# One tile for the edge buffers, and 34 gathers of a layer that take only the first rows of their block

## The chip, the cores and the metric

The kernel runs on one core of a Trainium2 chip. The metric is device time in microseconds (us) of one execution. Before the change it is 3410.35 us, the median of three runs (3400.02 to 3417.9). The profiled execution, a run of its own, took 3422.3 us, of which the profile's span covers 3420.5.

## The reference, cut to what matters

A graph of 6250 nodes with 128 features and 100,000 directed edges; each node has one of 16 types, each edge one of 32. Two layers of typed graph attention, then one linear layer, a residual and a layer norm:

```python
def gt_layer(x, ntype, etype, src, dst, Wk, Wq, Wv, Wa, Watt, Wmsg, pri, skip, g, b):
    k, q, v = (typed_linear(x, ntype, W).reshape(n, H, HS) for W in (Wk, Wq, Wv))
    kT = jnp.einsum('nhd,htdo->nhto', k, Watt)
    vT = jnp.einsum('nhd,htdo->nhto', v, Wmsg)
    a = jnp.einsum('ehd,ehd->eh', kT[src, :, etype], q[dst]) * pri[:, etype].T / SQRT_D
    att = edge_softmax(a, dst, n)
    hag = segment_sum((vT[src, :, etype] * att[:, :, None]).reshape(-1, H * HS), dst, n)
    h = silu(typed_linear(hag, ntype, Wa))
    alpha = sigmoid(skip[ntype])[:, None]
    return layer_norm(h * alpha + x * (1.0 - alpha)) * g + b
```

H is 8 heads of HS = 16. A softmax runs over the edges that arrive at one node, 16 of them on average.

## The kernel before

**Tables.** For each layer a table in device memory holds, for every node and edge type, one row of 256 numbers (1 KB): key and value after the edge type's matrices. PE makes it in pieces of 128 nodes by 16 edge types (`table_block`, L384), ScalarE and in part VectorE copy the pieces out of PSUM into `st` (L391, L389), and GpSimd (POOL in the profile) scatters each piece with an indirect DMA, rows of 16 KB (L537 for layer 0, L1997 for layer 1).

**Blocks and slots.** The nodes are sorted on the chip (`rank_order`): into four classes of four node types each, within a class by falling degree, and cut into blocks of 128 nodes, one node to a partition. Each block has a fixed number of slots, at most one edge of each node to a slot: 25, 21, 19, 18, 17, 16, 15, 15, 14, 12, 11 for the eleven blocks of a class (`OWN_SLOTS`) and 42, 20, 16, 14, 9 for five mixed blocks (`MIXED_SLOTS`), which take the nodes that found no room in their class. The first mixed block has 26 slots of its own and 2 that are shared. Since nodes are sorted by degree, a block's last slots are used by the nodes of its first partitions alone. `ell` holds for each node and slot the table row of its edge, fetched with one gather per block (L1139). In `limits_of`, `room` gets each block's number of slots by a memset (L1230), and if a degree is above it, `over` is set; the program then takes a general path, which walks the edges one at a time (`arm(False)`), in place of the fast one.

**The fast path's order.** `edges` runs once per layer over 16 superblocks of one to four blocks. A block's slots are cut into chunks of at most four (`CH`). Per chunk: `kv`, a buffer of 128 partitions by four slots by 256 numbers, one of 12 in a rotating pool (L1718); one indirect gather for each slot (L1722), which fetches 128 table rows by a column of `ell`; the product of the keys with the query (L1738, VectorE, all four slots at once, in place) and its sum per head into `a` (L1744). A block later the generator `finished` adds `neg`, which is -1e30 where a node has no edge in the slot, takes the softmax, weighs the values in place and adds them up over chunks (`kv<-kv,wq`, `acc<-kv,acc`); the last of these instructions gives the buffer back. 819 gathers a layer, 1638 in all.

**What sets the order.** In the fast path GpSimd's instructions stand in the written order. Those of the other engines are ordered by the framework, from dependencies, its own estimates and the edges drawn with `behind`: work of the nodes (`on.vector` and the like) stays behind the stream instruction that was written before it. That node work (typed linear layers, layer norm, next queries) and the pieces of the second table are generators, and `tick` advances them between chunks. GpSimd's queue thus holds gathers, the scatters of the second table (layer 0) and the scatters of the output (L2035, layer 1). A tile's dependencies and semaphores are drawn by the framework.

Of the kernel before, what the change touches and what calls it, by code (L numbers as in the profile page):

```python
# [9 lines left out]
F32 = mybir.dt.float32  # L10
# [4 lines left out]
ALU = mybir.AluOpType  # L15
# [4 lines left out]
P = 128  # L20
# [8 lines left out]
NC = 4  # L29
# [3 lines left out]
CH = 4  # L33
# [2 lines left out]

PIECE = 6


def bins_of_degrees(lam):  # L40

# [3 lines left out]

OWN_SLOTS = (25, 21, 19, 18, 17, 16, 15, 15, 14, 12, 11)
MIXED_SLOTS = (42, 20, 16, 14, 9)

# [27 lines left out]
def kernel(  # L78
# [21 lines left out]
    nc = tc.nc  # L100
    N, D = out.shape
# [11 lines left out]
    CB, MB = len(OWN_SLOTS), len(MIXED_SLOTS)  # L113
    KB = list(OWN_SLOTS) * NC + list(MIXED_SLOTS)
    NB = len(KB)
    MIXED0 = NC * CB * P
    NR = NB * P
    TOP = NC * CB
    GB = [OWN + REST if b == TOP else KB[b] for b in range(NB)]
    KO = [sum(GB[:b]) for b in range(NB)]  # L120
    KS = sum(GB)
# [21 lines left out]
    tabs = [dram.tile([(NR if l else NP) * RT, 2 * D], F32, name=f"tab{l}") for l in range(L)]  # L143
# [10 lines left out]
    ell = keep.tile([P, KS], I32, name="ell")  # L154
# [242 lines left out]
    pp = prep.enter_context(tc.tile_pool(name="prep", bufs=1))  # L397
# [26 lines left out]
    rowf = pp.tile([P, 1], F32, name="rowf")  # L424
# [73 lines left out]
    for e in range(AHEAD):  # L498
        nc.gpsimd.indirect_dma_start(
            out=xa[:, e, :], out_offset=None, in_=x,  # L500
            in_offset=bass.IndirectOffsetOnAxis(ap=ahead[:, e:e + 1], axis=0))
    nc.vector.tensor_tensor(toward, toward, firstmost.unsqueeze(2).to_broadcast([P, AHEAD, NT]),
                            op=ALU.not_equal)
# [4 lines left out]
    for tg in range(TG):  # L508
        nc.vector.tensor_scalar(ahead_rows[:, tg], ahead_f, float(TG), float(tg),
                                op0=ALU.mult, op1=ALU.add)  # L510
# [74 lines left out]
    for i in range(2):  # L585
# [5 lines left out]
                                 op0=ALU.mult, op1=ALU.add)  # L591
# [31 lines left out]
    for c0, i0 in enumerate(cuts[:3]):  # L623
# [11 lines left out]
        for i in range(sl.start, sl.stop):  # L635
            nc.vector.tensor_scalar(row1[:, i - i0], colb, placef[:, i:i + 1], None,
                                    op0=ALU.is_equal)
        for i in range(sl.start, sl.stop):
# [6 lines left out]
                            op0=ALU.mult, op1=ALU.add)  # L645
# [45 lines left out]
    for tg in range(TG):  # L691
        nc.vector.tensor_scalar(rows1[:, tg], place2, float(TG), float(tg),
                                op0=ALU.mult, op1=ALU.add)
# [9 lines left out]
                            op0=ALU.is_gt)  # L703
# [155 lines left out]
    with tc.If(unsorted > 0):  # L859
# [7 lines left out]
        with tc.For_i(0, EC, 1) as j:  # L867
# [7 lines left out]
                out=c0, out_offset=None, in_=cnt[:],  # L875
                in_offset=bass.IndirectOffsetOnAxis(ap=pair[:, 0:1], axis=0))
# [27 lines left out]
                out=cnt[:], out_offset=bass.IndirectOffsetOnAxis(ap=to[:, 0:1], axis=0),  # L904
                in_=c1, in_offset=None)
            nc.gpsimd.indirect_dma_start(
                out=order[:], out_offset=bass.IndirectOffsetOnAxis(ap=pos[:, 0:1], axis=0),
                in_=pair, in_offset=None)
# [9 lines left out]
    for r in range(N * RT, NR * RT, P):  # L918
        n = min(P, NR * RT - r)
        nc.sync.dma_start(tabs[1][r:r + n, :], zeros[:n])  # L920

    with tc.manual_schedule(engines={mybir.EngineType.Pool, *engines}):
# [246 lines left out]
        def limits_of(meta, full, rest_at):  # L1169
# [59 lines left out]
            for b in range(NB):  # L1229
                nc.vector.memset(room[:, b:b + 1], float(KB[b]))  # L1230
                if b % 4 == 3:
                    yield
            two = pp.tile([P, 2], F32, name="two")
            nc.vector.tensor_tensor(room, degr, room, op=ALU.is_gt)
            nc.vector.tensor_reduce(two[:, 0:1], room, axis=AX.X, op=ALU.max)
# [125 lines left out]
    def arm(fast):  # L1361
# [4 lines left out]
            on.hold()  # L1366

        outs_put, results = [], []
        STB = 3 if fast else 2
        ep = ctx2.enter_context(tc.tile_pool(name="ep", bufs=2))  # L1370
        npl = ctx2.enter_context(tc.tile_pool(name="npl", bufs=1))
        eps = npl.tile([P, 1], F32, name="eps")
        nc.vector.memset(eps, LN_EPS)
# [101 lines left out]
        def edges(l):  # L1475
# [201 lines left out]
            for s, (i0, k, types) in enumerate(sbs):  # L1677
                asked = None
                if s + 1 < len(sbs):
                    asked = queries(got, *sbs[s + 1])  # L1680
                    spread(work, asked, 24 if mixed(s + 1) else 11 if l == 0 else 8, asking(s))
                sums = ep.tile([P, SB, D], F32, name="sums")
                den = ep.tile([P, SB, H], F32, name="den")
                for i in range(k):
                    b = i0 + i
                    K = KB[b]
                    a = ep.tile([P, max(KB), H], F32, name="a")
                    own = OWN if b == TOP else K
                    chunks = [(j, min(j + CH, own)) for j in range(0, own, CH)]
                    if b == TOP:  # L1690
                        chunks.append((OWN, OWN + REST))
                    kvt = []
                    then = []

                    def steps():

                        for _ in range(2 if s + 2 >= len(sbs) else 1):
                            step()

                    def step(end=False):  # L1700

                        if next(before, then) is then and not then:
                            if i + 1 < k:
                                then.append(query(s, i + 1))
                            elif asked and (end or work == [] or all(w[0] is not asked
                                                                     for w in work)):
                                rush(work, asked)
                                then.append(query(s + 1, 0))

                    cut = 0  # L1710
                    if b == sbs[-1][0] + sbs[-1][1] - 1:
                        cut = (K - 2 * CH) // CH
                        assert cut > 0 and (K + 1) * H <= 2 * D and K < max(KB)
                    for j0, j1 in chunks:
                        c = j1 - j0
                        if b == sbs[-1][0] + sbs[-1][1] - 1 and j1 > K - 2 * CH:
                            closing.append(b)
                        kv = ep.tile([P, CH, 2 * D], F32, name="kv", bufs=12)  # L1718
                        kvt.append(kv)
                        for j in range(j0, j1):  # L1720
                            at = KO[b] + j
                            get = nc.gpsimd.indirect_dma_start(  # L1722
                                out=kv[:, j - j0, :], out_offset=None, in_=tabs[l][:],
                                in_offset=bass.IndirectOffsetOnAxis(ap=ell[:, at:at + 1], axis=0))
                            gathered[0] = True
                            if l == 1:
                                for put in puts:
                                    after(get, put, "rows of the table")
                                puts.clear()
                            elif at == KO[sbs[0][0]]:  # L1730
                                for load in load_next(nc.sync):
                                    after(load, get, "the first table goes first")
                        kk = kv[:, :c, :D]
                        rest = b == TOP and j0 == OWN
                        if rest:
                            moved(rows_of, got[s][0][:, i, :], kv[:, 2, :D])
                        of = kv[:, 2, :D] if rest else q
                        stream[nc.vector] = nc.vector.tensor_tensor(  # L1738
                            kk, kk, of.unsqueeze(1).to_broadcast([P, c, D]), op=ALU.mult)
                        steps()  # L1740
                        tick(c / 3)
                        to = (kv[:, 3, D:D + c * H].rearrange("p (k h) -> p k h", h=H) if rest
                              else a[:, j0:j1, :])
                        nc.vector.tensor_reduce(to, kk.rearrange("p k (h d) -> p k h d", h=H),  # L1744
                                                axis=AX.X, op=ALU.add)
                        if rest:
                            nc.vector.tensor_tensor(
                                kv[:, 3, :RK * c * H].rearrange("p (r c) -> p r c", r=RK),
                                nth.unsqueeze(2).to_broadcast([P, RK, c * H]),
                                kv[:, 3, D:D + c * H].unsqueeze(1).to_broadcast([P, RK, c * H]),  # L1750
                                op=ALU.mult)
                        if cut and len(kvt) == cut:
                            for _ in before:
                                pass
                            before = finished(s, i, chunks[:cut], kvt[:cut], a, sums, den,
                                              (0, j1))
                        steps()
                        tick(c / 3)
                        steps()
                        tick(c / 3)  # L1760
                        leave()
                    for _ in before:
                        pass
                    if not then:
                        step(end=True)
                    before = finished(s, i, chunks[cut:], kvt[cut:], a, sums, den,
                                      (chunks[cut][0], K) if cut else None)
                    q = then[0] if then else None
# [345 lines left out]
        if not fast:  # L2114
            for i0, k in superblocks(NT):
                n = k * P
# [87 lines left out]
```

## Time and profile before

| what | value |
|---|---|
| median of three runs | 3410.35 us |
| profiled execution | 3422.3 us |
| its span | 3420.5 us |
| busy: PE, DVE (VectorE), ACT (ScalarE), POOL (GpSimd) | 1793.1, 1867.6, 1019.3, 1975.8 us |
| gathers of L1722 | 1638, 1565.8 us busy |
| DMA | 672.23 MB, mean 197 GB/s |

A row of a group of instructions names line, engine, operation, output and inputs, count, busy time, mean duration in ns of one, and after the second bar the idle time of the engine just before them with what ended it ("issue" is time in which the engine waited for nothing that the profile shows, "remote" an event of which it knows no source). A row of waits names who waited, for whom, the total in us, how often, and the longest. A row of the timeline has start, duration, engine, line, operation, tiles and, in brackets, the idle time before it. A row of a line's own view gives the smallest, the median and the largest duration in ns. Many of VectorE's and PE's instructions stand under line 299, a helper, so they are told apart by their tiles. "PEld" is PE's weight load, "PEclk" the granted clock of TensorE.

### The profile page before, as it was taken

What the parts mean: (1) busy time and instruction counts of PE and PEld (TensorE: products, weight loads), DVE (VectorE), ACT (ScalarE), POOL (GpSimd) and SP (SyncE); (2) the same over time, 40 slices, a digit from 0 to 9 for tenths busy, and PEclk for the clock granted to TensorE, in tenths of its full rate; (3) what the DMA queues carried; (4) which work ended last, traced back from release to release, by engine and by line L of the source; (5) the groups of instructions that cost most, each with busy time, mean ns of one, the idle gap of its engine ahead of it and who ended that gap; (6) DMA issues with size and microseconds to landing.
All of it is one profiled execution on the core that took longest, in us unless ns stands there. A gap on an engine that the chain in (4) does not pass through costs nothing. (4 is left out here: it accounts for less than half of the span.)

```text
span 3420.5 us, 22378 instructions
## 1 busy us (share of the span) xinstructions
PE 1793.1 (52%) x5496; PEld 818.3 (24%) x5496; DVE 1867.6 (55%) x4420; ACT 1019.3 (30%) x2089; POOL 1975.8 (58%) x2123
## 2 busy tenths in 40 slices
PE   6999896118867678586877784011122103120122
PEld 3444333003324223232333342000011001010011
DVE  6576554446446555465555443456545645664566
ACT  5887343003432344333444453000101100010111
POOL 3334655665655655566656443756666566657664
PEclk8998766556667666776656675555555555555555
DMA  8999999335664566556767577323223333323231
GB/s 287 427 423 395 381 406 349 111 87 206 231 225 171 191 243 225 199 199 231 254 248 257 215 276 270 105 86 93 88 86 102 92 88 95 97 87 104 86 91 53
DMA packets 151156, 672.23 MB, mean 197 GB/s; under 512 B 35520, under 2 KB 67554, under 8 KB 125922
## 3 DMA queue, kind: packets, MB, share of 16 engines
q0 software_dynamic: 113472, 635.98, 51.8%
q1 hardware_dynamic: 32850, 31.51, 3.1%
q10 hardware_dynamic: 4688, 3.15, 0.4%
q8 instruction: 48, 0.79, 0.1%
q14 instruction: 98, 0.80, 0.1%
HBM read 245.49 MB, written 429.22 MB: 197 GB/s over the span
## 5 line engine op out<-in xcount | busy, mean ns | idle before, releaser
L1722 POOL DMA_INDIRECT kv<-tab,ell x1638 | 1565.8, 956 | 777.5 <-issue 461.5
L391 ACT COPY st<-tb 128x512 f32<-128x512 f32 x1371 | 727.4, 606 | 721.0 <-PE tb L384 397.1
L384 PE MATMUL tb<-bd,kvT 32*128 32x512 f32 x1538 | 591.4, 898 | 116.9 <-ACT st L391 62.9
L1738 DVE TENSOR_TENSOR kv<-kv,wq 128x512 f32<-128x512 f32 (+3 forms) x446 | 283.2, 637 | 242.1 <-DMA kv<-tab,ell 108.4
L299 PE MATMUL nb<-xm,wqa 128*128 128x384 f32 (+3 forms) x528 | 286.5, 703 | 166.8 <-issue 72.4
L1744 DVE TENSOR_REDUCE a<-kv 128x32 f32<-128x512 f32 (+3 forms) x446 | 282.4, 635 | 150.2 <-remote 95.8
L384 PEld LDWEIGHTS tb<-bd,kvT 32*128 32x128 f32 x1538 | 218.4, 246 | 351.3 <-issue 171.5
L299 DVE SCALAR_TENSOR_TENSOR xm<-ntb,nb 128x512 f32<-128x512 bf16 (+3 forms) x320 | 156.9, 543 | 229.0 <-remote 111.3
L1997 POOL DMA_INDIRECT tab<-st,row x98 | 97.1, 991 | 305.0 <-ACT st L391 224.0
L384 PE MATMUL tb<-bd,vT 32*128 32x512 f32 x800 | 250.6, 776 | 25.2 <-ACT st L391 10.6
L299 PE MATMUL nb<-xm,wkqv 128*128 128x384 f32 (+3 forms) x528 | 219.2, 572 | 65.9 <-issue 28.8
L299 DVE TENSOR_TENSOR acc<-kv,acc 128x512 f32<-128x512 f32 (+3 forms) x346 | 219.3, 634 | 62.7 <-remote 39.9
L299 PE MATMUL nb<-ident,hag 128*128 128x128 f32 x98 | 27.5, 417 | 406.3 <-DVE kv L1738 225.7
L299 PE MATMUL nb<-by,all_rows 49*128 49x512 bf16 (+3 forms) x32 | 14.5, 453 | 416.5 <-DVE kv L1738 207.0
L537 POOL DMA_INDIRECT tab<-st,rows x92 | 95.2, 1035 | 211.0 <-ACT st L391 178.5
L384 PE MATMUL tb<-bd,kT 32*128 32x512 f32 x800 | 212.5, 769 | 4.6 <-DVE st L389 4.1
L299 PEld LDWEIGHTS nb<-xm,wqa 128*128 128x128 f32 x528 | 134.6, 282 | 334.2 <-issue 204.9
L299 DVE TENSOR_TENSOR kv<-kv,wq 128x512 f32<-128x512 f32 (+3 forms) x334 | 207.7, 623 | 2.0 <-issue 2.0
L389 DVE COPY st<-tb 128x512 f32<-128x512 f32 x182 | 119.1, 686 | 111.9 <-PE tb L384 65.0
L299 PEld LDWEIGHTS nb<-xm,wkqv 128*128 128x128 f32 x528 | 112.7, 232 | 185.6 <-issue 92.5
L299 ACT ACTIVATE wq<-a 128x120 f32<-128x120 f32 (+12 forms) x98 | 28.4, 290 | 374.7 <-DVE xm L299 85.1
L1525 ACT COPY wq<-hq 128x128 f32<-128x128 f32 x49 | 13.1, 268 | 395.3 <-DVE acc L299 215.6
(387 smaller groups left out, 2020.8 us busy)
## 6 DMA issues: line engine op xcount, KB each, us to landing
kv<-tab,ell POOLq DMA_INDIRECT x1638
hq<-hqx SPq DMA_DIRECT2D x7, 768.0 KB
hqx<-hs SPq DMA_DIRECT2D x7, 512.0 KB
hq<-hqx SPq DMA_DIRECT2D x5, 576.0 KB
hqx<-xr SPq DMA_DIRECT2D x10, 256.0 KB
hqx<-hs SPq DMA_DIRECT2D x5, 384.0 KB
hr<-hqx SPq DMA_DIRECT2D x7, 256.0 KB
tab<-st,row POOLq DMA_INDIRECT x98
```

Of the source, the lines that this page charges most:

```text
L299: put = issue(*args, **kwargs)
L384: stream[nc.tensor] = nc.tensor.matmul(pt, yT[s, i * P:(i + 1) * P], bd[s, tt, :], start=True, stop=True)
L389: nc.vector.tensor_copy(to, pt)
L391: stream[nc.scalar] = nc.scalar.copy(to, pt)
L537: put = nc.gpsimd.indirect_dma_start(out=tabs[0].rearrange("(n t) c -> n (t c)", t=16), out_offset=bass.IndirectOffsetOnAxis(ap=rows_of_pi ...
L1525: nc.scalar.copy(standing["wq"][:, at:at + D], got[s][0][:, i, :])
L1722: get = nc.gpsimd.indirect_dma_start(out=kv[:, j - j0, :], out_offset=None, in_=tabs[l][:], in_offset=bass.IndirectOffsetOnAxis(ap=ell[:, ...
L1738: stream[nc.vector] = nc.vector.tensor_tensor(kk, kk, of.unsqueeze(1).to_broadcast([P, c, D]), op=ALU.mult)
L1744: nc.vector.tensor_reduce(to, kk.rearrange("p k (h d) -> p k h d", h=H), axis=AX.X, op=ALU.add)
L1997: put = nc.gpsimd.indirect_dma_start(out=tabs[1].rearrange("(n t) c -> n (t c)", t=16), out_offset=bass.IndirectOffsetOnAxis(ap=row2[:, tg ...
```

## The change

The twelve `kv` buffers become one tile `ring` of 48 slots, `RING * CH`; a chunk takes the next four in turn, counted by `fed` over both layers. Two tables of bounds name a block and a slot and give how many of the block's first nodes may use it: 7 for each of the four classes and 6 for the mixed blocks, 34 in all. In these slots a gather takes only that many rows (48 to 112, multiples of 16) and leaves the other partitions of the slot as they were; the first time that a slot of the ring is used, it takes all 128. In `limits_of` each bound lowers `room` by one for the nodes from the bound on, so that a node that would need such a slot sets `over`.

```diff
+RING = 12
...
+FEW = {(0, 22): 112, (0, 23): 80, (0, 24): 48, (1, 20): 112, (7, 14): 96, (8, 13): 112, (10, 10): 112}
+FEW_MIXED = {(1, 17): 112, (1, 18): 112, (1, 19): 112, (2, 13): 96, (2, 14): 96, (2, 15): 96}
...
+    few = {(c * CB + b, j): n for c in range(NC) for (b, j), n in FEW.items()}
+    few.update(((NC * CB + b, j), n) for (b, j), n in FEW_MIXED.items())
...
+            beyond = pp.tile([P, 1], F32, name="beyond")
+            for (b, j), n in few.items():
+                if b < CB or b >= TOP:
+                    nc.vector.tensor_scalar(beyond, rowf, float(n), None, op0=ALU.is_ge)
+                    nc.vector.tensor_tensor(room[:, b:b + 1], room[:, b:b + 1], beyond,
+                                            op=ALU.subtract)
+            for c in range(1, NC):
+                nc.vector.tensor_copy(room[:, c * CB:(c + 1) * CB], room[:, :CB])
+            yield
...
+        fed, filled = [0], set()
...
+        ring = ep.tile([P, RING * CH, 2 * D], F32, name="ring", bufs=1) if fast else None
...
-                        kv = ep.tile([P, CH, 2 * D], F32, name="kv", bufs=12)
+                        chunk = fed[0] % RING
+                        fed[0] += 1
+                        kv = ring[:, chunk * CH:(chunk + 1) * CH]
...
+                            n = few.get((b, j), P)
+                            if (chunk, j - j0) not in filled:
+                                filled.add((chunk, j - j0))
+                                n = P
                             get = nc.gpsimd.indirect_dma_start(
-                                out=kv[:, j - j0, :], out_offset=None, in_=tabs[l][:],
-                                in_offset=bass.IndirectOffsetOnAxis(ap=ell[:, at:at + 1], axis=0))
+                                out=kv[:n, j - j0, :], out_offset=None, in_=tabs[l][:],
+                                in_offset=bass.IndirectOffsetOnAxis(ap=ell[:n, at:at + 1], axis=0))
```

More of the change, by code (lines that the diff above doesn't have):

```diff
@@ L118 @@
     TOP = NC * CB
+    few = {(c * CB + b, j): n for c in range(NC) for (b, j), n in FEW.items()}
+    few.update(((NC * CB + b, j), n) for (b, j), n in FEW_MIXED.items())
+    assert all(n % 16 == 0 and j < KB[b] and (b, j - 1) not in few or few[b, j - 1] >= n
+               for (b, j), n in few.items())
+    assert all(j == KB[b] - 1 or (b, j + 1) in few for b, j in few)
     GB = [OWN + REST if b == TOP else KB[b] for b in range(NB)]
```

## The prediction

> **What bounds the kernel now.** I read the busy times by stage first, then the gathers' own line, then GpSimd's and VectorE's waits stage by stage, then the timeline at the places where a stage turns or ends. The stages are the preparation with the first table (0 to 580 us), the edges of layer 0 beside the second table (580 to 2080) and the edges of layer 1 (2080 to the end):
>
> ```profile
> core 0: us, PE busy (x) PEld busy (x) DVE busy (x) ACT busy (x) POOL busy (x), PEclk, DMA share, GB/s
> 0.00:580.00 580.00, 502.65 (x2189) 232.88 (x2189) 344.58 (x827) 341.61 (x669) 263.27 (x338) 0.81 0.96 386
> 580.00:2080.00 1500.00, 1044.39 (x2735) 461.99 (x2736) 783.52 (x1790) 543.93 (x1104) 876.23 (x914) 0.66 0.60 212
> 2080.00:3420.50 1340.50, 246.03 (x577) 123.40 (x571) 739.49 (x1805) 133.76 (x317) 836.28 (x872) 0.53 0.33 97
> ```
>
> The preparation is held by the DMA engines (share 0.96). In the other two stages no engine looks full. POOL's busy time leaves out what lies between its instructions, so I read that from the timeline:
>
> ```profile
> 1105.55 0.95 POOL L1722 DMA_INDIRECT kv<-tab,ell  x1 [0.30 <-issue]
> 1106.80 0.95 POOL L1722 DMA_INDIRECT kv<-tab,ell  x1 [0.30 <-issue]
> ...
> 2819.39 0.94 POOL L1722 DMA_INDIRECT kv<-tab,ell  x1 [10.18 <-DVE t L299]
> ```
>
> Gathers that wait for nothing start every 1.25 us: 0.95 in the instruction and 0.30 that always lies between two. With 0.30 for each instruction POOL is taken for 876.2 + 914 x 0.30 = 1150 of the 1500 us of layer 0 (77%) and for 836.3 + 872 x 0.30 = 1098 of the 1340.5 us of layer 1 (82%). It is the fullest engine of both, and what it lacks is waits such as the third line: a gather stood 10.18 us because VectorE had not yet let go of the buffer. By kind, layer 0 and then layer 1:
>
> ```profile
> POOL kv L1722 <- issue: 219.4, 718, 0.8
> POOL tab L1997 <- ACT st L391: 216.7, 40, 15.1
> POOL kv L1722 <- DVE acc L299: 75.8, 20, 16.2
> ```
> ```profile
> POOL kv L1722 <- issue: 225.4, 739, 0.6
> POOL kv L1722 <- DVE t L299: 70.3, 7, 16.3
> POOL kv L1722 <- DVE acc L299: 39.8, 9, 17.7
> POOL kv L1722 <- remote: 38.8, 15, 13.7
> ```
>
> In layer 0 the largest real wait is not of a gather: 216.7 us for ScalarE to fill a piece of the second table, which PE paces. In layer 1 it is 70.3 + 39.8 + 38.8 = 148.9 us in 31 waits for VectorE. The other direction, VectorE waiting for a gather to land, in layer 0 and then layer 1:
>
> ```profile
> DVE kv L1738 <- DMA kv<-tab,ell: 30.0, 14, 5.2
> ```
> ```profile
> DVE kv L1738 <- DMA kv<-tab,ell: 78.4, 30, 19.9
> ```
>
> So the two engines take turns: a stretch in which the gathers set the pace, then a chain of node operations in VectorE's queue during which the ring runs full and POOL stands. A gather made shorter pays only in a stretch of the first kind.
>
> **The change: what it saves on POOL.** A layer has 819 gathers; 34 become short. With the order of the superblocks and 48 slots used in turn, one of the first layer's (block 7, slot 14, 96 rows) falls on a slot that has never been filled and stays whole. That leaves 33 + 34 = 67 short gathers and 1008 + 1040 = 2048 fewer rows of 1638 x 128 = 209,664, just under 1%. What a row costs on POOL no line shows, since every gather before has 128. The nearest lines:
>
> ```profile
> L1722 POOL DMA_INDIRECT kv<-tab,ell x1638: 940/946/1828, 580.3 to 3391.8; - x182
> ```
> ```profile
> L1997 POOL DMA_INDIRECT tab<-st,row x98 | 97.1, 991 | 305.0 <-ACT st L391 224.0 <-issue 21.9 <-ACT rs L299 21.2
> L2035 POOL DMA_INDIRECT out_dram<-o,node x49 | 49.6, 1012 | 53.3 <-POOLq L2151 17.2 <-DVE kv L1738 15.3 <-issue 11.6
> L1139 POOL DMA_INDIRECT ell<-kvs,start x49 | 47.3, 965 | 16.4 <-issue 12.5 <-DMA tab<-st,rows 2.7 <-DVE alpha L1222 0.3
> L445 POOL MEMSET base_t<- 128x1 f32 x16 | 1.1, 88 | 0.0
> ```
>
> A kv gather takes 946 ns with rows of 1 KB, the ell gather 965 with rows of 36 to 104 bytes, the table scatter 991 with rows of 16 KB. Bytes cost nothing, so the 946 is a fixed part plus a part by rows. One end: all of it is by rows, 946 / 128 = 7.4 ns a row, 2048 x 7.4 = 15.1 us saved. (The memset of one column, 88 ns, shows that a POOL instruction need not have a large fixed part; with 88 fixed it would be 6.7 ns and 13.7 us.) Other end: all of it is fixed and a shape other than 128 rows costs a little, as the output scatter's 1012 does against 946: 67 x 0.066 = 4.4 us lost. All these rows have 128 rows and none lies nearer to either end, so I take the middle of fixed and by rows, 3.7 ns, which is 7.6 us less on POOL (3.7 in layer 0, 3.8 in layer 1).
>
> The Trainium skill, "DMA: Bandwidth & Descriptors", section "Anatomy of one DMA — SWDGE (gpsimd) path", speaks against this middle: it calls descriptor generation small and says that many descriptors can be emitted before their number shows. By that rule the gain on POOL is about nothing; no line of this trace, with 128 rows everywhere, can say which holds.
>
> **How much of it reaches the end.** In layer 0 POOL has 216.7 us of waits for table pieces, so a gain ahead of such a wait comes back as a longer one. In layer 1 148.9 us of waits for VectorE swallow what lies ahead of them, while the 78.4 us of VectorE's waits for landings give it out. The very end takes nothing:
>
> ```profile
> 3391.78 0.97 POOL L1722 DMA_INDIRECT kv<-tab,ell  x1 [0.30 <-issue]
> ...
> 3398.40 0.28 DVE L1738 TENSOR_TENSOR kv<-kv,wq 128x128 f32<-128x128 f32 x1
> ```
>
> The last three slots of the last block are short ones (112, 80, 48 rows), yet VectorE reaches the last of them 6.6 us after its gather starts and without waiting for it. Nor does the turn between the layers gain by a gather; layer 1 starts when the last table piece has landed:
>
> ```profile
> 2109.02 0.99 POOL L1722 DMA_INDIRECT kv<-tab,ell  x1 [11.53 <-DMA tab<-st,row]
> ```
>
> I let half pass, between none and all: 3.8 us.
>
> **The one tile.** Twelve chunks of four slots stay twelve chunks of four; the same bytes, and a chunk is given back by the same VectorE instruction as before. A gather could only lose if the waits were drawn for the whole tile and not by its parts. The index tile is already one tile filled by many gathers into columns, and they follow each other at the usual step, with no wait for the one before to land:
>
> ```profile
> 524.28 0.97 POOL L1139 DMA_INDIRECT ell<-kvs,start  x1 [0.97 <-DMA tab<-st,rows]
> 525.55 0.94 POOL L1139 DMA_INDIRECT ell<-kvs,start  x1 [0.30 <-issue]
> ```
>
> Waits already met cost POOL nothing either: 421 semaphore instructions of 17 ns stand ahead of gathers now, and they run inside the 0.95 us of the gather before (the step stays 1.25).
>
> ```profile
> L1722 POOLq EVENT_SEMAPHORE  x421: 17/17/43, 576.4 to 3351.8; - x141
> ```
>
> So I cost it at 0, from 0 up to the rivals below. VectorE's work over the slots is unchanged: products and sums still take all 128 partitions of a chunk.
>
> **The ranks' check.** Thirteen bounds give 26 operations on one column and 3 copies of 11 columns, in one burst at the place of the 49 memsets of `room`:
>
> ```profile
> L1230 DVE MEMSET room<- x49: 59/59/59, 347.9 to 394.6; 128x1 f32 x49
> ```
> ```profile
> 3414.11 0.16 DVE L299 TENSOR_TENSOR t<-t,v 128x1 f32<-128x1 f32 x1
> ```
> ```profile
> 300.00:400.00 100.00, 88.63 (x361) 41.27 (x360) 60.90 (x189) 50.18 (x97) 59.40 (x63) 0.77 0.98 398
> ```
>
> At 0.16 us that is 29 x 0.16 = 4.6 us on VectorE, which is busy 61 of 100 us there; the table copies queued behind it come late by that much once, and the scatters behind them, while the DMA engines (0.98) still work off earlier pieces. With that cover it costs 0, without it 4.6; I take 1.
>
> **Sum.** 3422.3 - 3.8 + 1.0 = 3419.5 us for an execution like the profiled one (span 3420.5 and 1.8 around it). That execution is 11.95 us above the median of the three runs, 3410.35, so against the median 3407.5; I say 3407. Bounds of the costs alone: -15.1 and +0 gives 3395; +4.4 and +4.6 gives 3419.
>
> **The rivals.** *The gather is flat*: 946 ns is per instruction, the rows are free, and only the burst of the check stays: 3411. For it: three very different row sizes have one duration, as if little but a fixed path were run. Against it: something must handle 128 indices. It is the Trainium skill's rule above.
>
> *All by rows, all reaching the end*: 3395. Against it: the 216.7 and 148.9 us of waits.
>
> *A new order of VectorE's queue, for the worse.* POOL's order is written out, but VectorE's, ScalarE's and PE's orders are laid out by the framework from dependencies and its own estimates, and twelve buffers turned into one tile, a changed gather and 29 more instructions alter what it works from. Place: the node chains of the superblocks, where POOL waits for VectorE's `t`, 70.3 us in 7 waits, 10.0 each. Two more such waits are 20 us, so 3407 + 20 = 3427 and three 3437; it decides from the second on. For it: only a few of the 16 chains of a layer hold POOL today, so others may. *The same the other way*: two such waits fewer, 3387.
>
> *The change does not do what it says*: if a node past a bound used its slot, the check would send the kernel to the general path, one edge at a time, far slower. Counted from the reference's inputs, block 0 of the first class uses its slots 22, 23, 24 for 58, 36 and 18 nodes, against 112, 80 and 48. Or waits for the whole ring: four gathers, landing and product took 2115.70 - 2109.02 = 6.7 us at the start of layer 1, and 448 chunks of that and the product one after the other come to over 3300 us for the two layers, against 2840 now.
>
> ```profile
> 2115.70 0.69 DVE L1738 TENSOR_TENSOR kv<-kv,wq 128x512 f32<-128x512 f32 x1 [19.93 <-DMA kv<-tab,ell]
> ```
>
> **How the numbers follow.** Forecast 3407: 0.38. Flat, 3411: 0.18. All by rows, 3395: 0.12. These three lie within 0.5% (3393 to 3427), which is about what a measurement of this kernel can tell from no change: 0.68. Better order, 3387: 0.17, faster. Worse order, 3427 and up: 0.13, and the failing cases 0.02: slower, 0.15. The range, 3380 to 3430, takes in the bounds of the costs, one worse order of two waits and most of the better order; it leaves out some 0.05 below and 0.12 above.
>
> **What would show it.**
>
> ```profile
> L1722 POOL DMA_INDIRECT kv<-tab,ell x1638 | 1565.8, 956 | 777.5 <-issue 461.5 <-DVE acc L299 115.6 <-DVE t L299 70.6
> ```
>
> Durations at the gather's line: a 48-row gather at 946 - 80 x 3.7 = 650 ns by my middle, 354 if all is by rows, 946 if flat, and the line's busy sum of 1565.8 us at 1558. POOL's step stays 1.25 us around whole gathers, and its semaphore instructions may multiply without moving it. POOL's waits for `t` and `acc` in layer 1 stay near 150 us; a sum off by 20 or more, with another order of VectorE's instructions, means the order rivals. The first 580 us stay within 5. I am wrong in kind if the two layers move by over 17 us, or if the preparation does.

## The result, and the profile after

The kernel became slower: 3426.92 us, the median of ten runs (3413.52 to 3445.22), beside 3407.63 us for ten runs of the kernel before on the same chip (3397.86 to 3417.9). The ratio is 1.006, with a 95% interval from 1.0036 to 1.0085. The profiled execution is the quickest of the ten, 3413.52 us (span 3411.6). It is shorter than the profiled execution of before (3422.3), so the two traces can't be subtracted as a whole; they must be read place by place. From each trace, in us:

| | before | after |
|---|---|---|
| first gather of layer 0 starts | 580.3 | 588.2 |
| from there to the first gather of layer 1 | 1528.7 | 1531.2 |
| from there to the last scatter of the output | 1306.2 | 1279.1 |
| from there to the end of the span | 5.3 | 13.2 |

The first and the last row turn out to be the ones that come back in the later runs. The two in the middle move by up to 15 us between three profiles of this one kernel, and by over 30 between all profiles of about 3400 us, so the prediction's mark of 17 us for the layers can't be read from one pair of traces. The busy times of the stages, as they were read before:

```profile
core 0: us, PE busy (x) PEld busy (x) DVE busy (x) ACT busy (x) POOL busy (x), PEclk, DMA share, GB/s
0.00:580.00 580.00, 499.08 (x2189) 237.87 (x2189) 350.20 (x854) 340.89 (x669) 262.65 (x338) 0.80 0.97 384
580.00:2080.00 1500.00, 1051.60 (x2695) 459.52 (x2696) 781.70 (x1782) 535.29 (x1086) 879.91 (x912) 0.67 0.59 210
2080.00:3411.60 1331.60, 259.17 (x614) 130.40 (x612) 738.67 (x1813) 142.46 (x335) 838.30 (x873) 0.54 0.33 100
```

The preparation has 27 more VectorE instructions and 5.6 us more of VectorE. POOL's busy time in the layers did not fall. The gathers' line on the page, and then in its own view (smallest, median and largest duration in ns, then the first and the last start):

```profile
L1749 POOL DMA_INDIRECT ring<-tab,ell x1638 | 1569.8, 958 | 755.4 <-issue 464.5
```
```profile
L1749 POOL DMA_INDIRECT ring<-tab,ell x1638: 868/949/2013, 588.2 to 3375.0; - x182
L1749 POOLq EVENT_SEMAPHORE  x423: 17/17/43, 584.2 to 3336.8; - x141
```

The busy sum rose from 1565.8 to 1569.8 us. The 67 short gathers are shorter, but only a little: the smallest is 868 ns. The median of all rose by 3 ns, which over 1638 gathers is 4.9 us and more than the rows gave; later profiles of the same kernel, and of others whose gathers are mostly whole, have 946 to 949 without a pattern that I could find. The semaphore instructions did not multiply (423 for 421), so waits for the whole ring are out. The waits in layer 0 and in layer 1:

```profile
POOL ring L1749 <- issue: 235.6, 727, 13.7
POOL tab L2024 <- ACT st L401: 190.3, 42, 14.4
POOL ring L1749 <- DVE acc L309: 70.3, 21, 10.7
```
```profile
POOL ring L1749 <- DVE acc L309: 44.1, 18, 17.0
POOL ring L1749 <- DVE t L309: 32.4, 5, 13.8
POOL ring L1749 <- remote: 24.8, 9, 12.5
```

In layer 1 the three kinds of wait sum to 101.3 us where they were 148.9. The prediction took a difference of over 20 us, together with another order of VectorE's instructions, for the mark of the order rivals. The order is the old one: set side by side, the lists of instructions of VectorE, PE, SP and GpSimd in the two layers are the same in both kernels, and on ScalarE one copy stands four places elsewhere. These waits differ between executions of the same order: two later profiles of the changed kernel have 125.2 and 124.4 us.

**The end.** The last scatter of the output, with the span of its execution, before and after:

```profile
core 0 of [0], span 3420.5 us
...
3415.19 1.00 POOL L2035 DMA_INDIRECT out_dram<-o,node  x1 [17.20 <-POOLq L2151]
```
```profile
core 0 of [0], span 3411.6 us
...
3398.39 0.99 POOL L2062 DMA_INDIRECT out_dram<-o,node  x1 [17.20 <-POOLq L2178]
```

After this instruction nothing is left to compute, yet the end comes 13.2 us later in place of 5.3. The trace's list of GpSimd's instructions names what fills it: an instruction called DRAIN near the end of GpSimd's queue, which the timeline leaves out. It began 2.7 us after the scatter and took 1.78 us before, and began 3.5 us after it and takes 8.88 us now. The scatter's packets have all landed by 3.0 us after its start in both. No term of the prediction had this place.

**The preparation.** VectorE after, from the start of the ranks' check to the copies queued behind it:

```profile
396.23 0.68 DVE L399 COPY st<-tb 128x512 f32<-128x512 f32 x1
396.83 0.15 DVE L1246 TENSOR_SCALAR beyond<-rowf 128x1 f32<-128x1 f32 x1
...
397.02 0.16 DVE L1247 TENSOR_TENSOR room<-room,beyond 128x1 f32<-128x1 f32 x1
...
401.72 0.31 DVE L1250 COPY room<-room 128x11 f32<-128x11 f32 x3
401.94 1.28 DVE L399 COPY st<-tb 128x512 f32<-128x512 f32 x2
```

The burst is nearly as forecast: 26 operations, all but one of 0.15 to 0.16 us, and three copies, 5.1 us from 396.83 to 401.94. The copies of the table behind it start late by that much, and PE, whose results they empty, with them. What this costs is told with the experiments.

### The profile page after: what moved, and what is told of

The parts are those of the page before. It is cut to its first block, busy times and chain, and to the rows that moved or that the text cites. A ratio compares the mean times of both kernels' runs of the same rounds, so it can differ in the third digit from the quotient of the medians.

```text
span 3411.6 us, 22407 instructions
## 1 busy us (share of the span) xinstructions
PE 1809.8 (53%) x5496; PEld 827.8 (24%) x5496; DVE 1870.6 (55%) x4449; ACT 1018.6 (30%) x2089; POOL 1980.9 (58%) x2123
## 5 line engine op out<-in xcount | busy, mean ns | idle before, releaser
L1749 POOL DMA_INDIRECT ring<-tab,ell x1638 | 1569.8, 958 | 755.4 <-issue 464.5
L394 PE MATMUL tb<-bd,kvT 32*128 32x512 f32 x1538 | 606.5, 895 | 135.7 <-ACT st L401 65.7
L1765 DVE TENSOR_TENSOR ring<-ring,wq 128x512 f32<-128x512 f32 (+3 forms) x446 | 282.4, 635 | 258.1 <-DMA ring<-tab,ell 119.9
L1771 DVE TENSOR_REDUCE a<-ring 128x32 f32<-128x512 f32 (+3 forms) x446 | 281.4, 633 | 118.8 <-remote 78.7
L2024 POOL DMA_INDIRECT tab<-st,row x98 | 98.8, 1008 | 295.9 <-ACT st L401 204.2
L309 PE MATMUL nb<-xm,wkqv 128*128 128x384 f32 (+3 forms) x528 | 227.5, 590 | 66.5 <-ACT kvT L309 46.4
L309 DVE TENSOR_TENSOR acc<-ring,acc 128x512 f32<-128x512 f32 (+3 forms) x346 | 218.5, 631 | 55.3 <-remote 33.8
L309 PE MATMUL nb<-by,all_rows 49*128 49x512 bf16 (+3 forms) x32 | 14.2, 445 | 395.6 <-DVE ring L1765 140.5
L309 DVE TENSOR_TENSOR ring<-ring,wq 128x512 f32<-128x512 f32 (+3 forms) x334 | 206.9, 621 | 2.0 <-issue 2.0
L309 PE MATMUL nb<-ident,hs 128*128 128x128 f32 x98 | 31.1, 453 | 220.7 <-DVE hs L309 219.6
```

The source lines that it names most:

```text
L309: put = issue(*args, **kwargs)
L394: stream[nc.tensor] = nc.tensor.matmul(pt, yT[s, i * P:(i + 1) * P], bd[s, tt, :], start=True, stop=True)
L1749: get = nc.gpsimd.indirect_dma_start(out=kv[:n, j - j0, :], out_offset=None, in_=tabs[l][:], in_offset=bass.IndirectOffsetOnAxis(ap=ell[:n ...
L1765: stream[nc.vector] = nc.vector.tensor_tensor(kk, kk, of.unsqueeze(1).to_broadcast([P, c, D]), op=ALU.mult)
L2024: put = nc.gpsimd.indirect_dma_start(out=tabs[1].rearrange("(n t) c -> n (t c)", t=16), out_offset=bass.IndirectOffsetOnAxis(ap=row2[:, tg ...
```

## The experiments

They ran on four chips. The kernel before took 3419.62, 3411.39, 2940.49 and 3413.54 us there (medians of 35, 35, 29 and 29 runs); why the third chip is so different is told further down. Comparisons are within a chip. Beside the ratio stands the difference of the means of all runs; its standard error is 2.6 to 4.2 us on the first, second and fourth chip and 0.6 to 1.0 us on the third.

### The parts one by one, first chip

The change again, and its two parts and one pair. The check alone keeps the lines of `limits_of` and the old buffers; the tile alone has

```diff
-                            n = few.get((b, j), P)
+                            n = P
```

and no check; the third has tile and short gathers and no check.

> The changed kernel once more, unaltered, beside three parts of it. If its loss is a property of the program, it comes out at about 1.006 of before again (some 20 us more), and a second profile shows which part of the 8 us later first gather (588.2 against 580.3 us) and of the layers holds. If the loss was the luck of those executions, it comes out within 0.3% of before.

> Before, with the ranks' check alone (29 more VectorE operations in the preparation, and the order of some 30 PE and VectorE instructions there that follows from them); buffers and gathers as before. Theory A, the check's burst sits on the preparation's path and all the loss begins there: the first gather of layer 0 comes 5 to 8 us later and the whole time is 8 to 20 us over before (1.002 to 1.006). Theory B, the ring does it: nothing here, within 0.2% of before.

> Before, with the one tile of 48 slots alone; every gather takes 128 rows and the ranks' check is as before. Theory A, the check does it: within 0.2% of before. Theory B, the one tile does it through the changed waits around the first mixed block (ScalarE's copies and PE's matmuls of the shared slots wait for other landings, one ScalarE copy moves by four places): 10 to 20 us over before (1.003 to 1.006), beginning at the fourth superblock of a layer.

> The change without the ranks' check: the one tile and the 67 short gathers. The short gathers save some 2 us of GpSimd by the profile of the changed kernel (868 to 926 against 943 ns), so by either theory it is the time of the one tile alone, within 0.2% of it. Theory A puts it at before's time, theory B at 10 to 20 us over it.

| | ratio (95%) | mean, us | first gather | last scatter to end |
|---|---|---|---|---|
| the change | 1.0043 (1.0019 to 1.0068) | +14.2 | 584.7 | 12.4 |
| the check alone | 1.0026 (1.0004 to 1.0049) | +6.0 | 590.3 | 5.9 |
| the tile alone | 0.9966 (0.9941 to 0.9992) | -9.1 | 580.7 | 5.4 |
| tile and short gathers | 1.0019 (0.9994 to 1.0044) | +9.1 | 585.0 | 12.4 |

The check is slower by itself, with a later first gather and the old end. A single first gather says little, though: tile and short gathers, without the check, have 585.0 us and the change itself 584.7, so the starts are compared over all profiles further down. The tile is not slower. The long end belongs to the short gathers: the DRAIN takes 1.78 us with the check alone, 2.01 with the tile alone, and 8.88 in both kernels that have the 67 short gathers.

### How many short gathers, second chip

One short gather alone, those of layer 0 alone, those of layer 1 alone, and a kernel whose ring is filled with 16 rows a slot in every second turn (the third kernel is the second edit with `l == 1`). The last one leaves the edges of the other 112 nodes of those slots out of the computation; all four leave out the check.

```diff
-                            n = few.get((b, j), P)
+                            n = few[b, j] if (l, b, j) == (0, 10, 10) else P
```
```diff
-                            n = few.get((b, j), P)
+                            n = few.get((b, j), P) if l == 0 else P
```
```diff
-                            n = few.get((b, j), P)
+                            n = 16 if fed[0] // RING % 2 else P
```

> The one tile, and a single short gather in the whole program (block 10, slot 10 of layer 0, 112 rows); the ranks' check as before. In the three kernels with short gathers GpSimd's last instruction, a DRAIN after the last output scatter, took 8.88 us against 1.78 to 2.01 in the three without. Theory C, a drain after any short gather is long: 8.9 us here too, and the time some 7 us over the one tile alone. Rival D, it grows with their number or follows where they leave the descriptors: 2 us here, and the one tile's time.

> The one tile, with the 33 short gathers of layer 0 alone; the ranks' check as before. The one tile with all 67 was 19 us slower than the one tile alone, 7 of them in the last drain. If the other 12 are real and arise where a gather is short, they split between the layers: this and the next kernel together lose 12 us besides their drains. If they were scatter of the runs (each median is good to some 3 us), this comes out at the one tile's time and its drain, at most 8 us over it.

> The one tile, with the 34 short gathers of layer 1 alone; the ranks' check as before. As for layer 0: 7 us of drain over the one tile if any short gather makes it long, and up to 12 more if the rest of the loss sits in layer 1; 7 in all if it does not.

> The one tile, with every second turn of the ring fetched with 16 rows a gather (the rows of the other 112 nodes stay as they were, so those nodes' edges are left out of the computation): about 810 short gathers. By the step of about 0.95 ns a row each is 106 ns shorter, 86 us of GpSimd in all. If half of what GpSimd saves reaches the end, as I had assumed, the time falls by 43 us against the one tile, less 7 of drain; if all, by 86 less 7; if the waits for VectorE and for the table pieces swallow it, by under 15. If short gathers have a cost of their own beside the drain (12 us by 67 of them), it shows here twelve times over: 140 us more.

| | ratio (95%) | mean, us | last scatter to end | DRAIN, us |
|---|---|---|---|---|
| one | 0.9996 (0.9972 to 1.002) | +0.1 | 5.8 | 1.77 |
| layer 0 (33) | 1.0003 (0.9979 to 1.0026) | -0.8 | 5.4 | 1.53 |
| layer 1 (34) | 1.0005 (0.9973 to 1.0038) | +0.5 | 5.1 | 1.11 |
| 16 rows, every second turn | 1.002 (0.9995 to 1.0046) | +9.4 | 14.0 | 10.59 |

One layer's short gathers cost nothing and bring nothing that can be measured, and the end stays short with them. The last kernel says the most. The gathers' groups of the tile alone and of this one:

```profile
L1740 POOL DMA_INDIRECT ring<-tab,ell x1638 | 1561.3, 953 | 733.8 <-issue 464.0
```
```profile
L1740 POOL DMA_INDIRECT ring<-tab,ell x1638 | 1481.6, 904 | 790.1 <-issue 451.2
```

The gathers' busy time is 79.7 us lower and POOL's idle time ahead of them 56.3 higher than in the tile alone on the first chip, and the kernel took 9.4 us more than before, of which 8 to 9 are the longer end. Of ten times the saving that the prediction had put on the change, nothing that can be measured reached the end.

### Twice the check, a spread check, other bounds, and the tile again, third chip

The check twice does every bound's pair of operations two times, with half a unit each; the spread one hands over to the table's instructions after every second bound:

```diff
+                if i % 2:
+                    yield
```

The third has the tile, all 67 short gathers at 112 rows, and no check.

> The ring and the 67 short gathers without the ranks' check, but every bound is 112 rows: 67 x 16 = 1072 rows fewer in all, about as few as in the runs with one layer's bounds alone (1008 and 1040), while the number of short gathers is that of the change. Where all 67 bounds stood, GpSimd's closing drain took 8.9 us and the time from the last output scatter to the end 12.4 to 13.2 us; with one layer's 33 or 34 bounds 1.1 to 1.5 and 5.1 to 5.4. Theory A (the rows left out in all decide, between 1040 and 2048): drain under 2.1 us, 5 to 6 us to the end, and a mean within 3 us of the kernel before. Theory B (the number of short gathers, between 34 and 67, decides): drain of 8.9 us and 12 to 13 us to the end, a mean some 7 us above. Either way the gathers of 112 rows take 930 to 935 ns.

> The ranks' check alone, with each bound's two operations done twice (half a unit each time, the same result): 52 one-column operations and 3 copies in one burst, some 10 us of VectorE in place of 5. Theory A (the burst is paid at the end of the preparation): the first gather starts 5 us later than with the check alone (584.7 to 590.3), so 590 to 595 us, and the mean is 8 to 13 us above the kernel before. Theory B (the burst is covered by the transfers and what the check alone showed, 6 us in the mean, is scatter between loaded programs): first gather at 580 to 590 and a mean anywhere from -5 to +6 us of the kernel before.

> The ranks' check alone, with a hand-over to the table's instructions after every second bound, so that four one-column operations (0.8 us) stand between two copies in place of 29. VectorE's work is the same. Theory A (the delay comes from the copies of the table queued behind one burst of 5 us): first gather back at 580 to 583 us, mean within 3 us of the kernel before. Theory B (VectorE's time itself, or the steps of the check that now come later, make the delay): first gather at 585 to 590 us, mean 4 to 8 us above.

> The one tile alone, a second time on other placement. It was 0.9966 (0.9941 to 0.9992) of the kernel before, 9 us less. If that gain belongs to the program: again 0.994 to 0.999. If it was scatter between loaded programs (the tile with one short gather was 0.9996): 0.998 to 1.002. Final drain near 2.0 us.

| | ratio (95%) | mean, us | first gather | last scatter to end |
|---|---|---|---|---|
| 67 bounds of 112 rows | 1.0019 (1.0009 to 1.0028) | +5.3 | 579.1 | 13.3 |
| the check twice | 1.0032 (1.002 to 1.0043) | +9.1 | 584.4 | 5.4 |
| the check spread | 1.0024 (1.0015 to 1.0033) | +7.1 | 581.9 | 5.6 |
| the tile alone | 0.9997 (0.9988 to 1.0006) | -1.0 | 576.4 | 6.2 |

The scatter between runs is much smaller here, so the small terms come out. The tile costs nothing; its 9.1 us less on the first chip did not come back. The doubled check, a burst of some 10 us, costs 9.1 us. It starts the first gather 8.0 us later than the tile alone, the spread one 5.5; against the other profile without the check (579.1) it is 5.3 and 2.8, so the starts alone would not decide. The times do: spreading did not take the loss away (7.1 us, where under 3 would have spoken for the burst). So it is not the length of one burst. That VectorE's time is what is missing fits both; that the check's later steps come later, which the expectation named beside it, was not tried by itself. Of the theories for the end, the one by rows fails as I had put it, since 1072 rows fewer in 67 gathers gave the long end (DRAIN 9.28 us), while 1040 in 34 had not; but a point between 1040 and 1072 rows would still fit, and the number of gathers too.

### The last four, fourth chip

The change a third time, the half-filled ring and the check a second time, and layer 1's 34 short gathers with 48 rows each, which leaves out the edges of the later nodes there:

```diff
-                            n = few.get((b, j), P) if l == 1 else P
+                            n = 48 if l == 1 and (b, j) in few else P
```

> The change itself once more. On a chip like the third (kernel before near 2940 us): the check 5.5 us, the closing drain 7 us, the rows 2 us back, so 10 to 12 us more than the kernel before, ratio 1.0034 to 1.0041. On one like the first two: 10 to 19 us more with scatter, as measured twice. Theory of my prediction in place of that (rows worth 7.6 us on GpSimd, check 1): the same or 4 us less.

> The ring, every second turn of it fetched with 16 rows (the edges of the other 112 nodes there are left out), 80 us less of gathers. Theory A (GpSimd sets the pace of the layers where VectorE is not late): on a chip like the third 60 to 80 us less than the kernel before, less the drain's 8, so 0.974 to 0.982; on one like the first two again -5 to +10 us. Theory B (the landings or VectorE's chains hold the layers on either chip): under 15 us less on any chip.

> The ranks' check alone. Theory A (its price is VectorE's time at a place where the table waits for VectorE, as check_twice with 9 us and the spread one with 7 us have it): 4 to 7 us more than the kernel before, first gather 4 to 9 us later than with the ring alone. Theory B (scatter): within 2 us.

> The ring and the 34 short gathers of layer 1 alone, every one with 48 rows (the edges of later nodes there are left out): 34 x 80 = 2720 rows fewer, as many short gathers as in the run with a drain of 1.1 us. Theory A (rows in all, a point between 1040 and 1072 fewer): closing drain of 8 to 10 us, 12 to 14 us from the last output scatter to the end. Theory B (the number of short gathers, or that both layers have them): drain under 2.1 us, 5 to 6 us to the end.

| | ratio (95%) | mean, us | first gather | last scatter to end |
|---|---|---|---|---|
| the change | 1.0048 (1.002 to 1.0075) | +16.7 | 590.5 | 12.4 |
| 16 rows, every second turn | 1.0008 (0.9985 to 1.003) | +2.1 | 581.6 | 14.0 |
| the check alone | 1.0022 (1.0 to 1.0044) | +5.7 | 589.8 | 5.8 |
| layer 1's 34 at 48 rows | one run, 3405.51 us | | 578.8 | 12.3 |

The check alone has its 5.7 us again. Where it goes is read from the transfers, in the tile alone (no check) and in the check alone, both on the first chip:

```profile
395.00:460.00 65.00, 59.73 (x194) 24.18 (x196) 33.13 (x70) 25.21 (x46) 39.81 (x45) 0.68 0.96 383
460.00:560.00 100.00, 82.96 (x331) 42.11 (x327) 56.02 (x107) 43.23 (x82) 62.60 (x67) 0.77 1.01 409
```
```profile
395.00:460.00 65.00, 52.90 (x173) 20.74 (x172) 36.95 (x107) 23.85 (x44) 36.98 (x41) 0.68 0.92 361
460.00:560.00 100.00, 84.20 (x326) 41.58 (x327) 55.10 (x107) 42.49 (x81) 58.99 (x62) 0.76 1.01 402
```

In the 65 us from the burst on, PE is busy for 52.9 in place of 59.7 us and the DMA engines move 361 in place of 383 GB/s, and 402 in place of 409 in the 100 us after. That holds over all profiles at 3400 us: a mean of 388 and 408 GB/s in the nine without the check and 371 and 402 in the five with it. 17 x 65 + 6 x 100 = 1.7 MB are left for later, 4.2 us at 405 GB/s; another 2.5 GB/s (383 for 380) is missing in the 395 us before, and is worth 2.4 us. The burst can't be its cause, since it comes later. The longer program moved some instructions of PE and VectorE against each other there, but that this is the cause isn't shown: four of the nine profiles without the check have 381 as well. Together the two are near the 7.2 us by which the first gather is late in the mean (588.7 in the five, 581.5 in the nine).

The last kernel separates rows from gathers. The last scatter and the span, with layer 1's own bounds (34 gathers, 1040 rows fewer) and with 48 rows in each of them (34 gathers, 2720 rows fewer):

```profile
core 0 of [0], span 3407.9 us
...
3402.79 0.99 POOL L2053 DMA_INDIRECT out_dram<-o,node  x1 [17.19 <-POOLq L2169]
```
```profile
core 0 of [0], span 3403.7 us
...
3391.40 0.99 POOL L2053 DMA_INDIRECT out_dram<-o,node  x1 [17.19 <-POOLq L2169]
```

The same gathers with fewer rows, and 12.3 us in place of 5.1 (DRAIN 8.96 for 1.11). The two ran on different chips, but a kernel's long DRAIN is the same from chip to chip (8.88 us in all three profiles of the change, 10.59 in both of the half-filled ring). So it is not the number of short gathers, and not that both layers have them; what is left is the rows. Their total sorts every profile: the end is short with 0, 16, 1008 and 1040 rows fewer and long with 1072, 2048, 2720 and far more. Whether that is a bound between 1040 and 1072, or something that repeats with the total, these eight values don't tell. What in GpSimd's closing work depends on that total isn't shown by any run.

## Why the prediction was wrong, step by step

The forecast was the same time or a little less; the kernel became slower. Two steps failed: the check's burst was taken as covered and put at 1 us, and cost 5.9; the very end was put at nothing, and cost 7.1. That the time lay in the range was luck: the upper part of the range was there for a worse order of VectorE's queue, which did not come.

**The gather's price by rows: wrong in size.** I took 3.7 ns a row, halfway between flat and 7.4. The last gathers of the kernel after, of 112, 80 and 48 rows, from the timeline:

```profile
3371.28 0.93 POOL L1749 DMA_INDIRECT ring<-tab,ell  x1 [0.30 <-issue]
3372.51 0.91 POOL L1749 DMA_INDIRECT ring<-tab,ell  x1 [0.30 <-issue]
...
3375.05 0.88 POOL L1749 DMA_INDIRECT ring<-tab,ell  x1 [0.30 <-issue]
```

The smallest of all are 943 ns with 128 rows and 868 with 48: 75 / 80 = 0.94 ns a row. The 7.6 us were 2048 x 0.94 = 1.9 us. The Trainium skill, "DMA: Bandwidth & Descriptors", section "Anatomy of one DMA — SWDGE (gpsimd) path", which calls descriptor generation small, was the better guide: by these rows it is 128 x 0.94 = 120 of 943 ns.

**Half of it reaches the end: wrong in kind.** The prediction read POOL as the fullest engine and let half pass, and 79.7 us less of gathers passed nothing that could be measured on two chips (+9.4 and +2.1 us, with 8 to 9 of the longer end in them). So on these chips neither POOL's time nor the transfers, whose packets were thinned as well, set the pace of the layers. What does isn't shown; the last section has a candidate for layer 1.

**The one tile at 0: right.** 0.9997 (0.9988 to 1.0006) where the scatter is smallest.

**The ranks' check at 1 us, 0 to 4.6: the cover failed.** The burst was sized rightly (4.6 us forecast, 5.1 measured). Wrong was the step by which the DMA engines, at a share of 0.98, would still work off earlier pieces. A share near 1 over 100 us did not mean that they had a stock: in the 65 us from the burst on they moved 17 GB/s less. Alone the check costs 6.0 and 5.7 us, and the five profiles with it have the first gather 7.2 us later in the mean than the nine without; the prediction's bound of 5 for the first stage holds in one of the five. The bound of 4.6 was too low already for the burst's own 5.1; whether the check costs more than its burst isn't settled, since the mean of 5.9 has a standard error of 1.9.

**The rivals.** On the gather the flat one was nearest, with 0.94 ns a row where all by rows would be 7.4. A worse order of VectorE's queue had the right sign by the wrong mechanism: the order in the layers did not change, which rules out the better order too. Waits for the whole ring, and the general path, are out (423 semaphore instructions; the same instructions run).

**What was not in it.** The closing DRAIN, 7.1 us longer. The prediction's sentence that "the very end takes nothing" looked at VectorE's last products and not at what GpSimd does after its last scatter.

**The sum.** The check 5.9, the end 7.1, the rows at most -1.9: 11 to 13 us. Measured for the change in the means: +21.7 in the first comparison (19.3 between the medians), then +14.2 and +16.7, with a standard error of some 3.7 each, so 17.4 with one of 2.1 together. The two named terms carry most of it; whether the remaining 4 to 6 us are scatter or a third term isn't settled. The short gathers without the check, +9.1 (first chip) and +5.3 (third), agree with an end of 7.1 and a saving of about 2.

## What to carry to other kernels

Before a saving on the fullest engine is counted, leave out a large part of that engine's work, even if the result is then incomplete, and see whether the end moves; here that one run was worth more than all rows of waits. A burst on an engine that feeds a stage bound by transfers need not be covered by their high share: here one of 5 us cost about 6 and one of 10 about 9, so look for a stock of finished pieces before counting it as covered. And read a trace to its very last instruction: what an engine does after its last useful work is part of the time, and a change far away can lengthen it.

## What the runs showed of the hardware that I had not expected

**A chip on which the same program takes 2940 us.** The windows of the three stages for the tile alone, on the first chip and then on the third:

```profile
0.00:580.00 580.00, 492.97 (x2189) 231.61 (x2189) 344.10 (x827) 340.39 (x669) 262.48 (x338) 0.81 0.96 386
580.00:2118.00 1538.00, 1052.23 (x2799) 465.88 (x2800) 790.44 (x1804) 555.35 (x1130) 878.75 (x917) 0.67 0.60 214
2118.00:3409.80 1291.80, 234.15 (x508) 116.17 (x507) 729.32 (x1791) 121.79 (x290) 829.60 (x868) 0.53 0.32 93
```
```profile
0.00:576.00 576.00, 486.69 (x2189) 234.85 (x2189) 344.37 (x827) 337.60 (x669) 262.52 (x338) 0.79 0.96 388
576.00:1814.00 1238.00, 949.08 (x2799) 444.06 (x2800) 789.51 (x1803) 545.33 (x1124) 880.37 (x917) 0.72 0.75 266
1814.00:2935.10 1121.10, 222.67 (x508) 116.21 (x507) 719.68 (x1791) 123.84 (x296) 831.55 (x868) 0.54 0.36 107
```

The preparation is alike, and so are VectorE's and POOL's busy times in the layers, yet layer 0 is 300 us shorter and layer 1 171, so it is their waits that are shorter. PE is busy for 103 us less in layer 0, at a granted clock of 0.72 in place of 0.67. On the third chip POOL is what the prediction took it for: in layer 1, 831.55 + 868 x 0.30 = 1092 of 1121 us.

**Instructions that wait for their own engine.** The same piece of VectorE's work in layer 1, on the first chip and on the third:

```profile
2217.80 0.28 DVE L309 TENSOR_TENSOR a<-a,neg 128x120 f32<-128x120 f32 x1
2218.00 0.54 DVE L309 TENSOR_TENSOR by<-tyr,ident 49x384 bf16<-49x384 bf16 x1
2220.59 0.69 DVE L1762 TENSOR_REDUCE a<-ring 128x32 f32<-128x512 f32 x1 [2.05 <-remote]
2221.99 0.37 DVE L309 TENSOR_REDUCE m<-a 128x8 f32<-128x120 f32 x1 [0.71 <-DVE a L1762]
```
```profile
1904.48 0.28 DVE L309 TENSOR_TENSOR a<-a,neg 128x120 f32<-128x120 f32 x1
1904.67 0.54 DVE L309 TENSOR_TENSOR by<-tyr,ident 49x384 bf16<-49x384 bf16 x1
1905.14 0.67 DVE L1762 TENSOR_REDUCE a<-ring 128x32 f32<-128x512 f32 x1
1905.74 0.35 DVE L309 TENSOR_REDUCE m<-a 128x8 f32<-128x120 f32 x1
```

The sum of `a` waits only for VectorE's own counter, that is for an earlier VectorE instruction, all of which had ended by 2218.54. On the first chip it starts 2.05 us late. Counted over the trace from 2080 us on: of 755 VectorE instructions with that one wait, 172 start over 0.3 us after their predecessor's end, 313 us in all and up to 7.0 us; of 509 with no wait at all, six do, for 3.0 us. In the preparation none does, and on the third chip none does anywhere. The fourteen profiles at about 3400 us all have them in layer 1, 172 to 200 for 313 to 367 us. Four in five of the late starts on the first chip follow the one before by a multiple of 0.70 us, to within 0.015 (2220.59 and 2221.99 are 1.40 apart), as if the counter were seen only at such steps. This is where I put the lost saving of the half-filled ring in layer 1; that it is the cause was not tried, since no edit of the kernel was found that takes them away, and no run of a half-filled ring fell on the third chip. For layer 0 it can't be: there the same fourteen profiles have 16 to 30 late starts for 28 to 53 us, while that layer is 300 us shorter on the third chip. What holds layer 0 stays open. The Trainium skill, "VectorE: DVE Perf Modes", section "The DRAIN you can't avoid", found no cost for a semaphore behind each of eight copies; on the third chip the trace agrees (none late), on the first it does not (313 us), and the measurement decides.

**"Issue" and "remote".** The same traces hold fewer records of semaphores: 8,109 increments by landed transfers for the tile alone on the first chip and 33,990 on the third. So a wait put down to "remote" or "issue" there may have had an ordinary cause whose record is missing, and the prediction's rows of waits in layer 1 were read from such a trace. Between chips, the landings are the wait that is seen: VectorE waited for them 93.4 us in layer 1 on the first and 376.8 on the third.

```profile
DVE ring L1756 <- DMA ring<-tab,ell: 93.4, 26, 20.0
```
```profile
DVE ring L1756 <- DMA ring<-tab,ell: 376.8, 159, 20.3
```
